# Products with M in one burst per group and layer, and another order of a network kernel's first microseconds

## The chip, the cores and the metric

The kernel runs on one core of a Trainium2 chip. The metric is device time in microseconds; lower is better. The kernel before was run four times: 3079.81, 3082.77, 3082.37 and 3082.63 us, median 3082.5 us.

## The reference

The input `x` holds 4 images of 32 by 32 positions and 16 channels, in float32. Four residual layers follow one another, each on a normalised copy of `x`:

```python
x = x + _L0_conv_ref(_gn(x), L0_conv_M, L0_conv_W, L0_conv_G)
x = x + _L1_conv_ref(_gn(x), L1_conv_M, L1_conv_W, L1_conv_G)
x = x + _L2_conv_ref(_gn(x), L2_conv_W0, L2_conv_b0, L2_conv_W1, L2_conv_b1, L2_conv_W2, L2_conv_b2)
x = x + _L3_conv_ref(_gn(x), L3_conv_M, L3_conv_Wp, L3_conv_G)
```

`_gn` normalises over the image and pairs of channels. Layers 0, 1 and 3 have the form

```python
first = jnp.einsum('ijyx,byxc->bijc', Msq, inputs)          # a 1024 x 1024 matrix
shifted = lax.conv_general_dilated(x_nchw, kern, STRIDES, PADDING)   # 1024*16 kernels of 3x3x16
diff = jax.nn.relu(inputs[:, None, None, :, :, :] - shifted)
second = L * jnp.einsum('ijyx,bijyxc->bijc', Wsq, diff)
return first - second
```

so that every output position has its own convolution of the whole image, whose result is weighed with a row of `W` and summed. Layer 2 is a pooling over intervals with two small dense steps; it matters here only as work beside the rest.

## The kernel before, in words

**Groups and phases.** The four images form two groups of two. The three big layers and two groups give six phases (L68), layer by layer, group 0 ahead of group 1. `conv_layer` (L431) works through one phase: 8 chunks of 128 output positions, 16 filters `f`, 2 images `b`, so 256 steps a phase and 1536 in all. A step is one PSUM tile `pc` of 128 by 1024: three slots of taps, each 64 rows deep in two halves that lie in different rows of the array (L457 to L467). Slots 0 and 1 multiply `raw` (the weights G as loaded, after a subtraction in place) with `im` (the shifted image, float32); slot 2 multiplies `W9` with `im9` (float32r). VectorE then clamps, weighs with the rows of W (tile `WT`) and sums, in one SCALAR_TENSOR_TENSOR `junk` (L471). There are three PSUM buffers for `pc`.

**Feeding.** A unit is 8 filters of a chunk (16 steps). `load_raw(u + 3)` is issued on SP's queue at step 2 of unit `u`, into four buffers; `prep(u + 1)` (L142) runs a tensor_tensor subtraction of `pick` on GpSimd (L150) and an ACT copy with a scale, `halve` (L123), and `prep_rest` adds VectorE's part, `halve_rest` (L126).

**Work beside the steps.** A generator `behind(phase)` (L487) holds the next phase's preparations; it is advanced by a count of steps that it yields itself. It holds the group norms, layer 2's `interval_layer` (L305: among others four transposes on VectorE L318, a scaled copy on ACT L322, a select on GpSimd L324), `before_conv` and `first_term` (L240), the products with M. The order of instructions on each engine is that of the recording; no scheduler rearranges them.

**The products with M.** `first_term` loads M of a layer in two halves of 2 MB (L247) into tile `MT`, which has one buffer. After a half is requested it waits 12 steps, then issues 32 products (4 tiles of 128 positions, 4 column strips of the array, each in two float32 passes; 16 program instructions), then requests the second half, waits 12 steps and issues the rest. Both halves add up in one PSUM bank `pf`. Two steps later VectorE transposes the bank and adds it to `X`. `first_term` is run six times.

**The first microseconds.** SP loads `XQ` (a copy of group 0 for the statistics), `im[0]` of image 0 in three transfers, one for each slot, the first `WT` chunk, the other six filters of the first `raw`, and image 1; ACT's queue loads the first two filters of `raw` (`F0 = 2`, L96). From `XQ` come the mean and the variance, each spread over the partitions by a product with `to_rows` (`first_stats`, L545, a multiply `by_batch` on VectorE and a product on TensorE). ACT takes the square root (L581), VectorE the reciprocal (L582), and then `normal` (L596: VectorE slots 0 and 1, ACT slot 2) and `sides` (L583: multiplications by 0 or 1 at the image's edges) make `im[0]`. The lines from L606 to L615 set the order. The first two filters are prepared by `prep(0, 0, F0, nc.vector)` (L579), ahead of the square root.

Of the kernel before, what the change touches and what calls it, by code (L numbers as in the profile page):

```python
# [8 lines left out]
F32 = mybir.dt.float32  # L9
# [5 lines left out]
P = 128  # L15
# [6 lines left out]
NT = NP // P  # L22
# [6 lines left out]
FU = 8  # L29
# [8 lines left out]
def net_kernel(ctx: ExitStack, tc: tile.TileContext, x, xq, xi, convs, iv_w, iv_b, out):  # L38
# [12 lines left out]
    nc = tc.nc  # L51
# [3 lines left out]
    wpool = ctx.enter_context(tc.tile_pool(name="wpool", bufs=2))  # L55
# [8 lines left out]
    def bank(name):  # L64
        return psum.tile([P, 512], F32, tag="one", bufs=2, name=name)
# [18 lines left out]
    def load_chunk(n):  # L84
        if n < n_chunks:
            t = n % NT
            chunks[n] = wpool.tile([P, NP], F32, tag="WT", name=f"WT_{n}")
            nc.sync.dma_start(chunks[n], convs[phases[n // NT][1]][1][t * P : (t + 1) * P, :])

    im = [const.tile([P, 3, GB, PITCH], F32, name=f"im{g}") for g in range(NG)]  # L90
# [2 lines left out]

    F0 = 2
    raws[0] = wpool.tile([P, 3, FU, P], F32, tag="raw", bufs=4, name="raw_0")
    nc.scalar.dma_start(raws[0][:, :, :F0], convs[0][2][0, 0][:, :, :F0])  # L96
    for slot in (0, 2, 1):
        nc.sync.dma_start(im[0][:, slot, 0], xi[0][:, slot])
    load_chunk(0)
    nc.sync.dma_start(raws[0][:, :, F0:], convs[0][2][0, 0][:, :, F0:])  # L100
    nc.sync.dma_start(im[0][:, :, 1], xi[1])
# [20 lines left out]
    def halve(dst, src, mask):  # L122
        nc.scalar.activation(dst, src, AF.Copy, scale=mask[:, 1:2])  # L123
# [15 lines left out]
        for y in (0, HP - 1):  # L139
            nc.gpsimd.dma_start(xs[g][:, y * HP : (y + 1) * HP], zero[:GC])  # L140

    def prep(u, at=0, to=FU, eng=nc.gpsimd):  # L142

        if u >= n_chunks * NU:
            return
        if at == 0:
            units[u] = (raws.pop(u), wpool.tile([P, FU, P], F32R, tag="W9", name=f"W9_{u}"))
        raw, W9 = units[u]
        f0 = u % NU * FU
        eng.tensor_tensor(  # L150
            raw[:, 1, at:to], raw[:, 1, at:to],
            pick[:, f0 + at : f0 + to].unsqueeze(2).to_broadcast([P, to - at, P]),
            ALU.subtract,
        )
        halve(W9[:, at:to], raw[:, 2, at:to], low_w)

    def prep_rest(u, at=0, to=FU):
        if u in units:
            raw, W9 = units[u]
            halve_rest(W9[:, at:to], raw[:, 2, at:to], low_w)  # L160
# [79 lines left out]
    def first_term(g, layer):  # L240


        xn = xns[g]
        ps = bank(f"pf_{g}{layer}")
        for half in range(2):
            mt = wpool.tile([P, NT // 2, 4, 256], F32, tag="MT", bufs=1, name=f"MT_{g}{layer}{half}")
            nc.sync.dma_start(mt, convs[layer][0][half])  # L247
            yield 12
            for k in range(NT // 2):
                pt = NT // 2 * half + k  # L250
                for j in range(4):
                    nc.tensor.matmul(  # L252
                        ps[32 * j : 32 * j + 32, :256], lhsT=xn[:, pt, :], rhs=mt[:, k, j, :],
                        start=pt == 0, stop=pt == NT - 1, tile_position=(0, 32 * j),
                    )
        yield 2
        ft = work.tile([P, NT * GC], F32, tag="fs", name=f"ft_{g}{layer}")
        nc.vector.transpose(ft, ps[:, : NT * GC])
        yield 1
        nc.vector.tensor_tensor(  # L260
            X[g], X[g], ft.rearrange("p (t m) -> p t m", t=NT), ALU.add
        )
        yield 1
# [167 lines left out]
    def conv_layer(phase, behind):  # L431
# [6 lines left out]
        for t in range(NT):  # L438
# [4 lines left out]
            for at, (f, b) in enumerate(steps):  # L443
# [3 lines left out]
                if at % (FU * GB) == (8 if u == 0 else 2):  # L447
                    prep(u + 1)
# [38 lines left out]
    def behind(phase):  # L487
        g, layer = phases[phase]
        if phase == 0:
            load_raw(1)  # L490
            load_raw(2)
            yield from rest_of_start()
            nc.scalar.dma_start(X[1], x[1])
            zeros(1)
            yield 1
            yield from constants()
        if phase + 1 < len(phases):
            g1, layer1 = phases[phase + 1]
            if layer1 == 2:
                yield from interval_layer(g1)  # L500
            yield from before_conv(g1, layer1)
            yield from first_term(g1, layer1)
        if phase == 0:
            yield from first_term(g, layer)
        if phase == len(phases) - 1:
            nc.sync.dma_start(out[1 - g], X[1 - g])
# [36 lines left out]
    s1 = const.tile([P, 1], F32, name="s1")  # L543

    def first_stats(src, name):  # L545

        ps = bank(f"ps_{name}")
        by_batch = work.tile([P, GB], F32, tag="by_batch", name=f"by_batch_{name}")
        nc.vector.tensor_scalar_mul(by_batch, own, src)
        nc.tensor.matmul(  # L550
            ps[:, :GB], lhsT=to_rows.rearrange("p k g s -> p (k g s)"), rhs=by_batch,
            start=True, stop=True,
        )
        return ps[:, :GB]

    nc.vector.tensor_reduce(s1, XQ, axis=AX.X, op=ALU.add)
    ps = bank("ps_own")
    nc.tensor.matmul(
        ps[:, :1], lhsT=to_own.rearrange("p q b c -> p (q b c)"), rhs=s1, start=True, stop=True
    )  # L560
    m = first_stats(s1, "m0")
    v = ident.rearrange("p (h q c) -> p q c h", h=2, q=4)
    nc.vector.tensor_reduce(pick, v[:, 0], axis=AX.X, op=ALU.add)
    low_w = rows_mask("low_w", ident.rearrange("p (h w k) -> p w h k", h=2, w=2)[:, 1:2])
# [9 lines left out]
    mean0 = const.tile([P, GB], F32, name="mean0")  # L574
    minus_mean0 = const.tile([P, GB], F32, name="minus_mean0")
    var = first_stats(s2, "v0")
    nc.vector.tensor_copy(mean0, m)
    nc.vector.tensor_scalar_mul(minus_mean0, m, -1.0)
    prep(0, 0, F0, nc.vector)  # L579
    rstd0 = const.tile([P, GB], F32, name="rstd0")  # L580
    nc.scalar.activation(rstd0, var, AF.Sqrt, bias=eps)  # L581
    nc.vector.reciprocal(rstd0, rstd0)  # L582
    def sides(eng, b, slot):  # L583

        v = im[0][:, slot, b].rearrange("p (y x) -> p y x", x=HP)
        if slot == 2:
            eng.memset(v[:, :, H - 1 : H], 0.0)
            eng.memset(v[64:, HI - 1, :H], 0.0)
        for side, at in (
            ("left", v[:, :, 0]), ("right", v[:, :, H - 1]),  # L590
            ("top", v[:, 0, :H]), ("bottom", v[:, HI - 1, :H]),
        ):
            if f"{side}{slot}" in keep:
                eng.tensor_scalar_mul(at, at, keep[f"{side}{slot}"])  # L594

    def normal(eng, b, slot):  # L596
        v = im[0][:, slot, b, :RUN]
        if eng is nc.scalar:
            eng.activation(v, v, AF.Identity, bias=minus_mean0[:, b : b + 1])
            eng.activation(v, v, AF.Copy, scale=rstd0[:, b : b + 1])  # L600
        else:
            eng.tensor_scalar(  # L602
                v, v, mean0[:, b : b + 1], rstd0[:, b : b + 1], op0=ALU.subtract, op1=ALU.mult
            )

    normal(nc.scalar, 0, 2)  # L606
    normal(nc.vector, 0, 0)
    sides(nc.vector, 0, 0)
    prep_rest(0, 0, F0)
    normal(nc.vector, 0, 1)  # L610
    sides(nc.vector, 0, 1)
    sides(nc.gpsimd, 0, 2)
    halve(im9[0][:, 0], im[0][:, 2, 0], low_x)
    halve_rest(im9[0][:, 0], im[0][:, 2, 0], low_x)
    prep(0, F0, FU)  # L615

    def rest_of_start():
# [92 lines left out]
```

## Time and profile before

| what | us |
|---|---|
| median of 4 runs | 3082.5 |
| profiled execution, its own time | 3079.81 |
| its span in the trace | 3078.1 |
| TensorE busy in the span | 3062.4 |
| VectorE busy | 2122.9 |
| GpSimd busy | 302.1 |
| ScalarE busy | 142.0 |

1.7 us of the profiled execution's time lie around the span. All four runs lie within 3.0 us, and the profiled one is the fastest of them. The page of the profile gives for each line its engine, its count, its busy time, the mean length of one and the idle time ahead of it with what ended it. The timeline gives a start, a length, an engine and a line for each instruction, in microseconds from the span's start. PEld is the weight load, which runs beside the products.

### The profile page before, as it was taken

What the parts mean: (1) busy time and instruction counts of PE and PEld (TensorE: products, weight loads), DVE (VectorE), ACT (ScalarE), POOL (GpSimd) and SP (SyncE); (2) the same over time, 40 slices, a digit from 0 to 9 for tenths busy, and PEclk for the clock granted to TensorE, in tenths of its full rate; (3) what the DMA queues carried; (4) which work ended last, traced back from release to release, by engine and by line L of the source; (5) the groups of instructions that cost most, each with busy time, mean ns of one, the idle gap of its engine ahead of it and who ended that gap; (6) DMA issues with size and microseconds to landing.
All of it is one profiled execution on the core that took longest, in us unless ns stands there. A gap on an engine that the chain in (4) does not pass through costs nothing.

```text
span 3078.1 us, 38112 instructions
## 1 busy us (share of the span) xinstructions
PE 3062.4 (99%) x15858; PEld 2071.1 (67%) x15858; DVE 2122.9 (69%) x3398; ACT 142.0 (5%) x145; POOL 302.1 (10%) x196
## 2 busy tenths in 40 slices
PE   8999999999999999999999999999999999999999
PEld 4555876758767766876775556685646578677776
DVE  6766666766666666666678776668877666666666
ACT  1000000000000000000000000000000000000000
POOL 3100000100000000000013310001330000000000
PEclk9999999999999999999999999999999999999999
DMA  3322112321111231111121113211113212121100
GB/s 144 126 103 77 67 48 76 99 95 49 52 72 48 71 125 71 53 55 62 48 76 48 69 59 116 76 48 61 57 48 126 76 48 71 48 76 49 69 28 2
DMA packets 36461, 215.20 MB, mean 70 GB/s; under 512 B 10432, under 2 KB 11456, under 8 KB 22592
## 3 DMA queue, kind: packets, MB, share of 16 engines
q1 hardware_dynamic: 29728, 207.65, 18.5%
q10 hardware_dynamic: 6432, 5.10, 0.7%
q8 instruction: 124, 2.03, 0.3%
q14 instruction: 49, 0.40, 0.0%
q0 software_dynamic: 128, 0.02, 0.0%
HBM read 211.77 MB, written 0.98 MB: 69 GB/s over the span
## 4 chain that ended last, share of the span: by engine, by line
PE 99%; DVE 0%; issue 0%; DMA 0%; ACT 0%; ACTq 0%
PE pc L461 98%; PE pf L252 1%; DVE junk L471 0%; DMA raw<-in_g 0%; PE ps_r L371 0%; PE ps_l L360 0%; DVE im L594 0%; PE ps_l L358 0%; DVE pp L318 0%; ACT L581 0%; ACT L123 0%; DVE im L602 0%; PE ps_y L422 0%; ACT W L123 0%; DVE W L126 0%
## 5 line engine op out<-in xcount | busy, mean ns | idle before, releaser
L461 PE MATMUL pc<-im,raw 64*128 64x512 f32 x12288 | 3001.5, 590 | 6.1 <-DVE im L594 4.3
L471 DVE SCALAR_TENSOR_TENSOR junk<-pc,WT 128x1024 f32<-128x1024 f32 x1536 | 1879.0, 1223 | 945.4 <-PE pc L461 939.9
L461 PEld LDWEIGHTS pc<-im,raw 64*128 64x128 f32 x12288 | 1712.5, 186 | 746.7 <-issue 425.8
L461 PE MATMUL pc<-im,W 64*128 64x512 f32 x3072 | 1709.5, 806 | 0.0
L461 PEld LDWEIGHTS pc<-im,W 64*128 64x128 f32 x3072 | 484.7, 186 | 227.6 <-issue 165.1
L150 POOL TENSOR_TENSOR raw<-raw,pick 128x1024 f32<-128x1024 f32 (+1 forms) x96 | 181.4, 1891 | 1918.4 <-DMA raw<-in_g 1790.0
L123 ACT ACTIVATE W<-raw,low_w 128x1024 fp32r<-128x1024 f32 (+1 forms) x97 | 110.6, 1140 | 2464.3 <-PE pc L461 2464.3
L126 DVE SCALAR_TENSOR_TENSOR W<-raw,low_w,W 128x1024 fp32r<-128x1024 f32 (+1 forms) x97 | 135.0, 1391 | 0.0
L471 DVE DVE_READ_ACCUMULATOR junk<-pc,WT 128x1 f32 x1536 | 126.7, 82 | 0.0
L391 POOL TENSOR_TENSOR dp_a<-ft_a,rt_r 128x1089 f32<-128x1089 f32 x16 | 39.0, 2446 | 75.5 <-DVE s_a L398 49.5
L391 POOL TENSOR_TENSOR dp_b<-ft_b,rt_r 128x1089 f32<-128x1089 f32 x16 | 37.1, 2324 | 94.6 <-ACT ft_b L384 47.7
L252 PE MATMUL pf<-MT,xn 128*32 128x256 f32 x384 | 23.2, 382 | 0.0
L182 POOL PARTITION_ALL_REDUCE sum_mc<-part_mc x6 | 2.7, 445 | 195.7 <-DVE part_mc L175 189.9
L398 DVE TENSOR_REDUCE s_b<-dp_b 128x33 f32<-128x1089 f32 x16 | 20.5, 1283 | 0.0
L398 DVE TENSOR_REDUCE s_a<-dp_a 128x33 f32<-128x1089 f32 x16 | 20.5, 1282 | 0.0
L252 PEld LDWEIGHTS pf<-MT,xn 128*32 128x32 f32 x384 | 11.3, 109 | 13.1 <-issue 6.9
L483 DVE TENSOR_TENSOR X<-X,acc 128x32 f32<-128x32 f32 x48 | 11.8, 247 | 1.5
L123 ACT ACTIVATE im<-im,low_x 128x1088 fp32r<-128x1088 f32 (+1 forms) x7 | 7.5, 1073 | 114.6 <-DMA im<-xs 110.3
L182 POOL PARTITION_ALL_REDUCE sum_mi<-part_mi x2 | 0.9, 445 | 116.6 <-DVE part_mi L175 116.6
L338 DVE TENSOR_TENSOR pp<-pp 64x1024 f32<-64x1024 f32 x10 | 12.1, 1212 | 0.0
L333 DVE TENSOR_TENSOR pp<-pp 64x1024 f32<-64x1024 f32 x10 | 12.1, 1211 | 0.0
L182 POOL PARTITION_ALL_REDUCE sum_vc<-part_vc x6 | 2.6, 441 | 88.4 <-DVE part_vc L175 82.4
(102 smaller groups left out, 141.4 us busy)
## 6 DMA issues: line engine op xcount, KB each, us to landing
raw<-in_g SPq DMA_DIRECT2D x95, 1536.0 KB, 6.6
WT<-in_w SPq DMA_DIRECT2D x48, 512.0 KB, 6.4
MT<-in_mt SPq DMA_DIRECT2D x12, 2048.0 KB, 7.8
im<-xs SPq DMA_DIRECT2D x60, 67.8 KB, 3.1
im<-xs ACTq DMA_DIRECT2D x60, 67.8 KB, 3.2
raw<-in_g SPq DMA_DIRECT2D x1, 1152.0 KB, 7.8
im<-in_xi SPq DMA_DIRECT2D x3, 272.0 KB, 4.5
im<-in_xi SPq DMA_DIRECT2D x1, 816.0 KB, 9.2
```

Of the source, the lines that this page charges most:

```text
L123: nc.scalar.activation(dst, src, AF.Copy, scale=mask[:, 1:2])
L126: nc.vector.scalar_tensor_tensor(dst, src, mask[:, 0:1], dst.bitcast(F32), op0=ALU.mult, op1=ALU.add)
L150: eng.tensor_tensor(raw[:, 1, at:to], raw[:, 1, at:to], pick[:, f0 + at : f0 + to].unsqueeze(2).to_broadcast([P, to - at, P]), ALU.subtract,)
L182: nc.gpsimd.partition_all_reduce(m, part, channels=P, reduce_op=bass_isa.ReduceOp.add)
L252: nc.tensor.matmul(ps[32 * j : 32 * j + 32, :256], lhsT=xn[:, pt, :], rhs=mt[:, k, j, :], start=pt == 0, stop=pt == NT - 1, tile_position= ...
L333: nc.vector.tensor_tensor(pp[k][:, :H, M:], a[:, :H, M:], a[:, s : H + s, M:], ALU.max)
L338: nc.vector.tensor_tensor(pp[k][:, :H, M:], a[:, :H, M:], a[:, :H, M - s : M - s + H], ALU.max)
L391: nc.gpsimd.tensor_tensor(t, ft[:, i, :].unsqueeze(1).to_broadcast([P, T1, T1]), rt, ALU.add,)
L398: nc.vector.tensor_reduce(s[:, i - 1, :], last, axis=AX.X, op=ALU.max)
L461: nc.tensor.matmul(ps[:, h, :], lhsT=w[:, f % FU, :], rhs=v[:, :, :H], start=slot == 0, stop=slot == 2,)
L471: nc.vector.scalar_tensor_tensor(junk, ps.rearrange("p h n -> p (h n)"), 0.0, chunks[n], op0=ALU.min, op1=ALU.mult, accum_out=acc[:, t, co ...
L483: nc.vector.tensor_tensor(X[g][:, t], X[g][:, t], acc[:, t], ALU.add)
```

## The change

Two things are changed.

`first_term` has one tile `MT` for the whole M of a layer, twice as large and still with one buffer. Both halves are requested one after the other, then 24 steps pass, then all 64 products are issued in one go. The count of steps up to the end of `first_term` (28) is the same.

The first microseconds are ordered differently. Image 0 comes in one transfer of 816 KB instead of three of 272 KB. The variance's product stands ahead of the mean's; the mean's `by_batch` multiply moves behind the variance's. The subtraction for the first two filters goes from VectorE to GpSimd, and `prep(0, 0, F0)` with its ACT copy stands behind the square root and not ahead of it. VectorE does slot 0 and slot 1 with their sides first and `prep_rest(0, 0, F0)` after them.

```diff
+    nc.sync.dma_start(im[0][:, :, 0], xi[0])
     nc.scalar.dma_start(raws[0][:, :, :F0], convs[0][2][0, 0][:, :, :F0])
-    for slot in (0, 2, 1):
-        nc.sync.dma_start(im[0][:, slot, 0], xi[0][:, slot])
...
-        eng.tensor_tensor(
+        nc.gpsimd.tensor_tensor(
...
+        mt = wpool.tile([P, NT, 4, 256], F32, tag="MT", bufs=1, name=f"MT_{g}{layer}")
+        for half in range(2):
+            nc.sync.dma_start(mt[:, NT // 2 * half : NT // 2 * (half + 1)], convs[layer][0][half])
+        yield 24
         ps = bank(f"pf_{g}{layer}")
-        for half in range(2):
-            mt = wpool.tile([P, NT // 2, 4, 256], F32, tag="MT", bufs=1, name=f"MT_{g}{layer}{half}")
-            nc.sync.dma_start(mt, convs[layer][0][half])
-            yield 12
-            for k in range(NT // 2):
-                pt = NT // 2 * half + k
-                for j in range(4):
-                    nc.tensor.matmul(
-                        ps[32 * j : 32 * j + 32, :256], lhsT=xn[:, pt, :], rhs=mt[:, k, j, :],
-                        start=pt == 0, stop=pt == NT - 1, tile_position=(0, 32 * j),
-                    )
+        for pt in range(NT):
+            for j in range(4):
+                nc.tensor.matmul(
+                    ps[32 * j : 32 * j + 32, :256], lhsT=xn[:, pt, :], rhs=mt[:, pt, j, :],
+                    start=pt == 0, stop=pt == NT - 1, tile_position=(0, 32 * j),
+                )
...
-    m = first_stats(s1, "m0")
...
     var = first_stats(s2, "v0")
+    m = first_stats(s1, "m0")
     nc.vector.tensor_copy(mean0, m)
     nc.vector.tensor_scalar_mul(minus_mean0, m, -1.0)
-    prep(0, 0, F0, nc.vector)
...
+    prep(0, 0, F0)
     normal(nc.scalar, 0, 2)
-    normal(nc.vector, 0, 0)
-    sides(nc.vector, 0, 0)
+    for slot in range(2):
+        normal(nc.vector, 0, slot)
+        sides(nc.vector, 0, slot)
+    sides(nc.gpsimd, 0, 2)
     prep_rest(0, 0, F0)
-    normal(nc.vector, 0, 1)
-    sides(nc.vector, 0, 1)
-    sides(nc.gpsimd, 0, 2)
```

More of the change, by code (lines that the diff above doesn't have):

```diff
@@ L140, in zeros, with prep @@
             nc.gpsimd.dma_start(xs[g][:, y * HP : (y + 1) * HP], zero[:GC])
-    def prep(u, at=0, to=FU, eng=nc.gpsimd):
+    def prep(u, at=0, to=FU):
         if u >= n_chunks * NU:
```

## The prediction

> **What bounds the kernel now.** I read the page first, then the chain of work that ended last, then timelines of three places: the start, a burst of M products, and the one place where TensorE waited after the start.
>
> ```profile
> span 3078.1 us, 38112 instructions
> PE 3062.4 (99%) x15858; PEld 2071.1 (67%) x15858; DVE 2122.9 (69%) x3398; ACT 142.0 (5%) x145; POOL 302.1 (10%) x196
> ...
> PE 99%; DVE 0%; issue 0%; DMA 0%; ACT 0%; ACTq 0%
> ```
>
> TensorE is the bound all along: 99% of the chain is its own. Only two things move the time: what TensorE does per step or burst, and the 15.7 us (3078.1 - 3062.4) in which it does nothing. Of those, some 12.5 lie ahead of 13.18 us; 1.8 lie at 2106 us; the rest is VectorE's last step.
>
> The start, from the timeline (start, length, engine, line):
>
> ```profile
> 5.60 1.28 ACT L123 ACT_TABLE_LOAD   x1 [5.60 <-DMA raw<-in_g]
> ...
> 6.20 0.59 PE L550 MATMUL ps_v<-by_batch_v,to_rows 128*128 128x2 f32 x2 [1.23 <-DVE by_batch_v L549]
> ...
> 6.90 0.51 ACT L123 ACTIVATE W<-raw,low_w 128x256 fp32r<-128x256 f32 x1
> ...
> 7.42 1.28 ACT L581 ACT_TABLE_LOAD   x1
> ...
> 8.72 0.26 ACT L581 ACTIVATE rstd<-ps_v,eps 128x2 f32<-128x2 f32 x1
> ...
> 10.53 2.08 PE L461 MATMUL pc<-im,raw 64*128 64x512 f32 x4 [3.74 <-DVE im L594]
> ...
> 11.17 1.50 POOL L150 TENSOR_TENSOR raw<-raw,pick 128x768 f32<-128x768 f32 x1 [0.41 <-DMA raw<-in_g]
> ...
> 11.37 1.75 DVE L594 TENSOR_SCALAR im<-im,kept 128x16 f32<-128x16 f32 x3
> ...
> 13.18 2.08 PE L461 MATMUL pc<-im,raw 64*128 64x512 f32 x4 [0.57 <-DVE im L594]
> ```
>
> The variance is ready at 6.79 (6.20 + 0.59), but ACT takes its root at 8.72: ahead of it in ACT's order stand the copy for the first two filters and a second table load, because that copy comes first and loads another table. The first three sides of slot 1 take 1.75 us, those of slot 0 took 0.66: the first of the three (1.33 us by its line's longest) ends when GpSimd's subtraction ends. So slot 0's products start at 10.53 and slot 1's, from which on TensorE runs without a break, at 13.18.
>
> A burst of M (VectorE's steps around it; the same distances stand at the other eleven, within 0.4 us where VectorE had extra work):
>
> ```profile
> 168.46 1.22 DVE L471 SCALAR_TENSOR_TENSOR junk<-pc,WT 128x1024 f32<-128x1024 f32 x1 [0.72 <-PE pc L461]
> ...
> 170.30 1.45 PEld L252 LDWEIGHTS pf<-MT,xn 128*32 128x32 f32 x32 [0.57 <-issue]
> ...
> 170.42 1.22 DVE L471 SCALAR_TENSOR_TENSOR junk<-pc,WT 128x1024 f32<-128x1024 f32 x1 [0.73 <-PE pc L461]
> ...
> 172.17 0.30 PEld L461 LDWEIGHTS pc<-im,raw 64*128 64x128 f32 x4 [0.41 <-issue]
> ...
> 174.44 1.22 DVE L471 SCALAR_TENSOR_TENSOR junk<-pc,WT 128x1024 f32<-128x1024 f32 x1 [2.79 <-PE pc L461]
> ```
>
> A step without a burst is 1.96 us (168.46 to 170.42), one with it 4.02 (170.42 to 174.44): a burst costs 2.06.
>
> **Part 1, M in one burst.** Nothing is taken out of the sum of products: 384 stay 384. The chain of waits gives 1.86 us for each 32, so 2.06 - 1.86 = 0.20 us is what going in and out of a burst costs. In the order of the built program the 64 products of a group and layer stand in a row, so six of twelve such changes go: 6 x 0.20 = **1.2 us less**. Ends: 0, and from the weight loads' idle time around a burst (0.57 + 0.41, less twice the 0.24 that a step has anyway, 0.5) 6 x 0.5 = 3.0. I take 0.2, for it is measured on the path.
>
> The loads: 2 MB land 7.8 us (median) after issue, at worst 11.2, both halves so in about 16 to 22 us, and the burst is 24 x 1.96 = 47 us behind. The halves stand on SP's queue ahead of a WT or a raw load, which they delay by as much; a raw load is issued at step 2 of unit u and used at step 2 of u + 2, 63 us later. If this cover were gone, TensorE would wait for the landing itself, up to 11 us a group; the margin is 25 us. On the other hand SP no longer stands waiting for the first 32 products (58.8 us in three waits up to 300 us now); behind it stood raw loads with the same 63 us of room, so this is worth nothing. VectorE is empty handed for 3.7 us in a row and not twice 1.9; it waits 0.73 a step anyway. PSUM: the bank is taken later and given back at the same step.
>
> **Part 2, the first microseconds.** With the root first, ACT has one table load, which waits for nothing in the new order and lies at about 1.5 to 2.8 us. VectorE's `by_batch` for the mean (0.23 long, 0.20 on its neighbours) moves behind the variance: by_batch of the variance is due at 5.72 instead of 5.92. But GpSimd now does the subtraction of the first two filters when they land, at 5.60; by its row for 768 columns (1.50) that is 0.50, and a small VectorE multiply may stand until it ends, as the sides at 11.37 did: I take 6.1. Then, with the rows' lengths and 0.05 between engines: 0.23 + 0.05 + 0.59 to the variance, root at 7.0 to 7.3; beside it the mean's multiply 0.23, its product 0.59, the copies 0.2 to 8.15; the reciprocal 0.17 to 8.3. VectorE's order makes the mean the later of the two now. From the start of `normal` to the first product it was 1.32 (9.21 to 10.53), so slot 0's products start at 9.6. Image 0's transfer is needed at 8.2; its three parts landed within 4.6 us of issues up to 2.2, one transfer of the same bytes ahead of the same others in the same queue should be there by 7.
>
> Slot 1 is then `normal` 0.56 and sides 0.66 behind slot 0's, at 10.8, ahead of the landing of raw's rest at about 11.1, which starts GpSimd's long subtraction: the 1.33 us hold is gone. TensorE needs slot 1 after two pairs at the slow clock, 2 x 0.855 (the distance of weight loads up to 18.89), at 11.3. Slot 2 needs ACT's two passes from 8.2 (1.52 long), GpSimd's clearing 0.35, ACT's copy 0.75 and VectorE's 0.48 + 0.78: about 12.0; it is due at 13.0. Now slot 0 is done in 1.71 and TensorE goes on without a break from 9.6.
>
> The clock: weight loads come every 0.855 us up to 18.89 and every 0.43 after about 19.2, 6.0 after the unbroken start at 13.18. At 19.2 before has done 1.71 + 5.9 = 7.6 us of work at the slow clock. With 6.0 again, after is at full clock at 15.6, with 6.0 done; the other 1.6 takes 0.8: level at 16.4, so **2.8 us less**. Ends: if the clock counts from the first product (10.53 to 19.2 is 8.7), 1.4 less; if it takes only the 3.65 us of the restart shown below, 4.0 less; if GpSimd holds VectorE by as much as in that place (3.0 us more than usual) when the variance is due, slot 1 comes at 13.9 and 0.7 us is lost. I take 2.8, as the nearest row is the same start.
>
> A rule beside a row: here the load at 7.42 takes 1.28, and the root follows at 8.72. The Trainium skill, "ScalarE: Activation LUTs", "What ACT_TABLE_LOAD costs", has 1283 ns for the load and some 1380 more for a drain at each switch of sets. By that page the switch that goes would be worth 1.4 more, and the whole some 5.4 instead of 4.0; the row shows no such drain, and I go by the row.
>
> **Sum.** 1.2 + 2.8 = 4.0 less: 3079.81 becomes 3075.8 for an execution like the profiled one. That one is 2.7 below the median; I take the 4.0 off the median: **3078.5 us**. That is no more than 0.13%; 0.2%, or 6.2 us, is about what a measurement of this kernel can tell from no change.
>
> **What may lie over it.** One place explains why runs differ by 2.7:
>
> ```profile
> 1588.88 1.28 DVE L126 SCALAR_TENSOR_TENSOR W<-raw,low_w,W 128x1024 fp32r<-128x1024 f32 x1
> 1588.93 2.37 POOL L324 TENSOR_SCALAR_AFFINE_SELECT pp<-pp 64x1024 f32<-64x1024 f32 x1 [15.15 <-ACT pp L322]
> ...
> 2102.40 4.27 DVE L126 SCALAR_TENSOR_TENSOR W<-raw,low_w,W 128x1024 fp32r<-128x1024 f32 x1
> 2102.45 1.27 POOL L324 TENSOR_SCALAR_AFFINE_SELECT pp<-pp 64x1024 f32<-64x1024 f32 x1 [15.10 <-ACT pp L322]
> ...
> 2107.87 3.65 PE L461 MATMUL pc<-im,raw 64*128 64x512 f32 x8 [1.76 <-DVE junk L471]
> ```
>
> In group 1's interval layer VectorE and GpSimd start within 0.05 us of one another and VectorE loses: 4.27 instead of 1.28. TensorE stands still 1.76 us and comes back at half clock (0.50 to 0.53 of it up to 2111.5). In group 0 the same pair went the other way and cost nothing. From 2098.30 to 2153.00 there are 26 steps, 54.70 - 26 x 1.962 = 3.7 us lost. The change doesn't touch this place, but each execution may lose here none, once or twice.
>
> **The rivals.**
> *One loss fewer:* if the runs of the changed kernel lose 3.7 us once where the median of before lost it twice, 3078.5 - 3.7 = 3074.8, faster. For it: 0.05 us decides, and the four runs differ by about such a step. Against: the order at this place is the same, so the same odds.
> *The start brings nothing:* the mean's later product and GpSimd's hold eat what the table load gives. Only M's 1.2 is left: 3081.3. For it: the 4.27 row; against: 1.93 us between variance and root are gone at once.
> *M brings nothing,* as the array's change of shape is hidden or is paid by the product: 3079.7. That the burst isn't one is excluded by the built order.
> *Slower:* a burst of 3.7 us lowers TensorE's clock. The products with M use 32 columns and rows of 256 elements and may count as little activity; a burst of 1.9 is maybe too short for it. Price: after the stall the clock was at half for 3.65 us, 1.8 us lost; six times, 11.0: 3078.5 + 11.0 = 3089.5. It turns the sign from 0.7 us a burst, and 0.2% from 1.7. Against: the granted clock is 1.00 in every window around the bursts, and the step after a burst is as short as others (174.44 to 176.41). The trace has no burst of 3.7.
> The row says that a stand of 1.76 us was enough. The Trainium skill, "TensorE: Matmul & The Clock Gate", "What's actually happening", wants about 3.4 us of an idle window for a drop and as much of a busy one for the way back; a burst of 3.7 would be longer than its window and two of 1.9 are not, so if that page's monitor saw the bursts as idle, it would speak against this change with about that price.
>
> **How the numbers follow.** Forecast 3078.5: 0.50. One loss fewer, 3074.8: 0.20. Start without gain, 3081.3: 0.17. M without gain, 3079.7: 0.07. Slower, 3089.5: 0.06. Faster by over 0.2% (below 3076.3) is the second alone: 0.20; slower by over 0.2% (above 3088.7) the last: 0.06; within it the rest: 0.74. The range takes in all but the last: from 3074.8 less 0.8 for the start's better end, 3074.0, to the start's worse end (0.7 lost, 1.2 won, 3082.0) and some of the runs' own spread, 3083.0.
>
> **What would show it.** One table load ahead of 5 us; the root by 7.3; slot 0's products by 9.6 and no wait of TensorE up to the second step; full clock by about 15.6 (3.4 us earlier). Bursts of 64, 3.72 long, with one gap; a step with a burst 5.9 us instead of 4.0 twice, and clock 1.00 after it. L126 at the two interval layers: 1.28 or 4.27 tells how many losses the execution had. I am wrong if TensorE waits at a burst, if the clock drops after one, or if slot 0's products come later than 10.5.

## The result, and the profile after

The changed kernel takes **3077.0 us** (median of 34 runs, 3072.2 to 3078.28) against 3082.2 us (54 runs, 3076.8 to 3083.5) of the kernel before: ratio 0.9983, 95% interval 0.9978 to 0.9988, so 5.2 us or 0.17% less. Forecast were 3078.5 us and 4.0 us less.

The profiled execution of the changed kernel took 3076.75 us. The page's head:

```profile
span 3075.0 us, 38107 instructions
...
PE 3059.2 (99%) x15858; PEld 2005.2 (65%) x15858; DVE 2126.4 (69%) x3397; ACT 141.1 (5%) x144; POOL 301.4 (10%) x197
```

TensorE is the bound as before. The start, in the timeline of the changed kernel (start, length, engine, line):

```profile
1.47 1.28 ACT L578 ACT_TABLE_LOAD   x1 [1.47 <-PEq L695]
...
5.14 0.61 POOL L149 TENSOR_TENSOR raw<-raw,pick 128x256 f32<-128x256 f32 x1 [3.56 <-DVE XQ L565]
5.16 0.87 DVE L568 SCALAR_TENSOR_TENSOR squares<-XQ 128x256 f32<-128x256 f32 x1
...
6.99 0.26 ACT L578 ACTIVATE rstd<-ps_v,eps 128x2 f32<-128x2 f32 x1 [4.23 <-PE ps_v L548]
...
7.90 0.16 DVE L575 COPY mean<-ps_m 128x2 f32<-128x2 f32 x1 [0.68 <-PE ps_m L548]
...
8.23 0.56 DVE L599 TENSOR_SCALAR im<-im,mean,rstd 128x542 f32<-128x542 f32 x1
...
9.55 3.78 PE L459 MATMUL pc<-im,raw 64*128 64x512 f32 x8 [1.69 <-DVE im L591]
...
13.41 1.88 PE L459 MATMUL pc<-im,raw 64*128 64x512 f32 x8
```

One table load is left, off the path; the root comes 1.7 us earlier (8.72 before); slots 0 and 1 are one group of eight products, without the break before 13.18. What takes the root's place as the last to come is the mean (7.90). Beside GpSimd's subtraction VectorE's `squares` is 0.87 long (0.42 before, where GpSimd has no work there). The weight loads reach their short distance, the sign of the full clock, at 13.4. The fourth step's first weight load is at 17.09, before at 20.95: 3.86 us.

The first burst of M in the same trace, with VectorE's steps around it:

```profile
188.08 1.23 DVE L469 SCALAR_TENSOR_TENSOR junk<-pc,WT 128x1024 f32<-128x1024 f32 x1 [0.35 <-PE pc L459]
...
189.93 3.18 PEld L250 LDWEIGHTS pf<-MT,xn 128*32 128x32 f32 x64 [0.57 <-issue]
...
190.04 1.22 DVE L469 SCALAR_TENSOR_TENSOR junk<-pc,WT 128x1024 f32<-128x1024 f32 x1 [0.73 <-PE pc L459]
...
195.79 1.22 DVE L469 SCALAR_TENSOR_TENSOR junk<-pc,WT 128x1024 f32<-128x1024 f32 x1 [4.52 <-PE pc L459]
```

From 190.04 to 195.79 it is 5.75, less a step of 1.96: a burst of 64 costs 3.79, two of 32 cost 4.12. That is 0.33 a group and layer, 2.0 for six. The table by stretches has the burst in its second row and the steps after it in its third (length, busy time of the engines, granted clock, DMA share, GB/s):

```profile
186.00:189.90 3.90, 3.90 (x22) 1.62 (x18) 2.97 (x5) 0.00 (x0) 0.00 (x0) 1.00 0.00 0
189.90:193.50 3.60, 3.60 (x66) 1.98 (x64) 1.23 (x2) 0.00 (x0) 0.00 (x0) 1.00 0.02 5
193.50:197.40 3.90, 3.90 (x24) 1.97 (x22) 1.23 (x2) 0.00 (x0) 0.00 (x0) 1.00 0.71 227
```

TensorE is busy throughout, its clock stays at 1.00, and the next step takes the usual 1.96 (195.79 to 197.75). The moments at which the granted clock changes, which the trace keeps, lie at none of the six bursts: the rival of a clock that falls after a long burst is gone.

The table of waits of the changed kernel (us in all, times, longest) and the timeline show that this execution lost at both interval layers, the profiled one of before only at the second:

```profile
PE pc L459 <- DVE junk L469: 3.5, 2, 1.8
```

```profile
1583.60 4.27 DVE L125 SCALAR_TENSOR_TENSOR W<-raw,low_w,W 128x1024 fp32r<-128x1024 f32 x1
1583.64 1.27 POOL L322 TENSOR_SCALAR_AFFINE_SELECT pp<-pp 64x1024 f32<-64x1024 f32 x1 [15.35 <-ACT pp L320]
1584.90 1.89 POOL L149 TENSOR_TENSOR raw<-raw,pick 128x1024 f32<-128x1024 f32 x1
...
1589.07 2.76 PE L459 MATMUL pc<-im,raw 64*128 64x512 f32 x8 [1.77 <-DVE junk L469]
```

VectorE's instruction is recorded 0.04 us ahead of GpSimd's, and ends only after two of GpSimd's. Counting 26 steps on from 1579.49 (to 1634.25) gives 54.76 - 26 x 1.962 = 3.75 us lost; from 2097.19 (to 2150.26) 2.06. The two differ by the clock, here after the first and after the second stand (what decides is in the last section):

```profile
1591.00:1592.00 1.00, 1.00 (x4) 0.45 (x4) 0.69 (x2) 0.00 (x0) 0.00 (x0) 0.50 0.00 0
...
2108.00:2109.00 1.00, 1.00 (x8) 0.55 (x6) 0.90 (x3) 0.00 (x0) 0.00 (x0) 1.00 0.00 0
```

So the spans add up roughly: -3.86 (start) - 2.0 (bursts) + 3.75 + 2.06 - 3.7 (two losses instead of one) = -3.75; measured -3.1 (3078.1 to 3075.0). By the first interval layer the two traces agree with it to 0.1 us (VectorE's transposes start at 1580.64 instead of 1585.93, 5.29 less). The other 0.7 us lie right behind it, at the interval layer's products `ps_r`: the 15 steps of VectorE around them take 31.62 us before (1633.86 to 1665.48) and 32.43 after (1632.28 to 1664.71). What makes them dearer the traces don't show.

### The profile page after: what moved, and what is told of

Same layout as the page of the kernel before. It is cut to its first block, busy times and chain, and to the rows that moved or that the text cites. A ratio compares the mean times of both kernels' runs of the same rounds, so it can differ in the third digit from the quotient of the medians.

```text
span 3075.0 us, 38107 instructions
## 1 busy us (share of the span) xinstructions
PE 3059.2 (99%) x15858; PEld 2005.2 (65%) x15858; DVE 2126.4 (69%) x3397; ACT 141.1 (5%) x144; POOL 301.4 (10%) x197
## 4 chain that ended last, share of the span: by engine, by line
PE 99%; DVE 1%; issue 0%; POOL 0%; POOLq 0%
PE pc L459 98%; PE pf L250 1%; DVE junk L469 0%; PE ps_r L369 0%; PE ps_l L358 0%; DVE pp L316 0%; PE ps_l L356 0%; DVE squares L568 0%; PE ps_y L420 0%; DVE im L591 0%; PE ps_m L548 0%; PE ps_v L548 0%; DVE im L599 0%; DVE kept L539 0%; DVE to_own L523 0%
## 5 line engine op out<-in xcount | busy, mean ns | idle before, releaser
L459 PEld LDWEIGHTS pc<-im,raw 64*128 64x128 f32 x12288 | 1681.5, 186 | 705.8 <-issue 424.4
L459 PE MATMUL pc<-im,W 64*128 64x512 f32 x3072 | 1659.0, 806 | 0.0
## 6 DMA issues: line engine op xcount, KB each, us to landing
MT<-in_mt SPq DMA_DIRECT2D x12, 2048.0 KB, 11.6
```

Source lines behind the costliest of these rows:

```text
L459: nc.tensor.matmul(ps[:, h, :], lhsT=w[:, f % FU, :], rhs=v[:, :, :H], start=slot == 0, stop=slot == 2,)
```

## The experiments

My theory: both parts gain, M by fewer changes of burst and the start by the root; over them lies the meeting of VectorE and GpSimd in the interval layers, which costs an execution 0, 2.1 or 3.7 us at each of two places. Rivals: all of it is the start; all of it is fewer losses; the long burst costs clock. Twelve kernels ran, in three sets of four, each set on one chip (another one each time) with the kernel before beside it, which had medians of 3079.89, 3082.44 and 3082.18 us. To take the meeting away, "shifted" kernels move the interval layer's transposes, copy and select two steps later and keep all that follows in place:

```diff
             nc.gpsimd.memset(t, -BIG)
-        yield 3
+        yield 5
...
-        yield 4
+        yield 2
         k = 0
```

| kernel | median us (range, runs) | ratio to before, 95% interval |
|---|---|---|
| e1 M alone | 3076.37 (3073.17 to 3079.8, 11) | 0.9987, 0.9979 to 0.9996 |
| e2 start alone | 3077.32 (3073.72 to 3081.5, 11) | 0.9989, 0.9980 to 0.9997 |
| e3 before, shifted | 3075.85 (3075.21 to 3076.3, 11) | 0.9984, 0.9975 to 0.9993 |
| e4 changed, shifted | 3071.18 (3070.38 to 3072.42, 6) | 0.9970, 0.9958 to 0.9981 |
| e5 M alone, shifted | 3073.89 (3072.89 to 3074.66, 8) | 0.9973, 0.9963 to 0.9983 |
| e6 start alone, shifted | 3073.29 (3072.32 to 3074.67, 7) | 0.9974, 0.9963 to 0.9984 |
| e7 = e4, M in quarters | 3076.37 (3075.51 to 3077.74, 11) | 0.9982, 0.9973 to 0.9991 |
| e8 = e4, mean first | 3071.02 (3069.93 to 3071.69, 5) | 0.9964, 0.9952 to 0.9977 |
| e9 = e4, three transfers | 3070.33 (3069.53 to 3071.36, 5) | 0.9964, 0.9952 to 0.9977 |
| e10 = e8, three transfers | 3069.59 (3069.3 to 3070.9, 5) | 0.9963, 0.9950 to 0.9975 |
| e11 = e3, root first | 3072.17 (3071.42 to 3072.85, 6) | 0.9969, 0.9958 to 0.9981 |
| e12 = e3, slots first | 3074.65 (3073.35 to 3075.73, 11) | 0.9978, 0.9969 to 0.9987 |

**e1, M alone.** The diff of `first_term` without the rest.

> Only the products with M are changed: one tile for the whole matrix, one burst of 64 per group and layer; the first microseconds are as before. My theory (a change of burst costs TensorE a fixed time, and both parts add up): a step with a burst is 5.75 us in the trace, as in the changed kernel, and twice 4.02 in the kernel before, so 0.33 x 6 = 2.0 us less than before: 3080.2 median; clock 1.00 after each burst. Rival A (the gain is all in the start): within 0.5 us of before. Rival B (the long burst lowers the clock): longer by 1.8 us a burst, 11 us.

3.5 us less, with an interval of 1.2 to 6.5: the part gains by itself, rivals A and B fall. For its size the interval is too wide.

**e2, start alone.** The rest of the diff, `first_term` as before.

> Only the first microseconds are changed; M is multiplied in two bursts as before. My theory: slot 0's products start at 9.5 to 9.6 us and TensorE goes on without a break; 1.4 to 4.0 us less than before, by the moment at which the clock rises; median 3079.3, that is 2.9 less. Rival A: all of the changed kernel's 5.2 us. Rival C (the difference is one of collisions in the interval layers alone): within 0.5 us of before once the two places are counted out.

2.6 us less, interval 0.9 to 6.2. This too gains by itself; that it isn't all of the 5.2 the interval doesn't show (e5 and e6 do). Its runs lie 7.8 us apart, and its profiled execution lost once (1.8 us of waiting), that of e1 twice (3.5).

**e3 and e4, the shift.** The diff above, on the kernel before and on the changed one.

> The kernel before, with the interval layer's transposes, scaled copy and select two steps later (yield 3 becomes 5, and the yield after the select 4 becomes 2, so that all that follows stands where it stood). My theory: VectorE's L126 and GpSimd's select no longer meet, L126 is 1.28 us in both places, TensorE doesn't wait after the start; one or two losses of 2.1 to 3.75 us go, so 3 to 6 us less than before, median 3077.5, and the runs lie closer together. Rival (the 4.27 us come from another cause than the meeting, or move to the next place): the time stays within 1 us of before.

> The changed kernel with the same two steps' shift. My theory: what the shift gives adds to what the change gives, so as much under the changed kernel as the shifted kernel before is under the kernel before, 3 to 6 us: median 3072.5; and it stands under the shifted kernel before by 2.0 (bursts) + 1.4 to 4.0 (start) = 3.4 to 6.0. Rival C (the change gives its time only by fewer collisions): within 1 us of the shifted kernel before.

The theory holds. In e3's timelines of VectorE and of GpSimd the two are 5 us apart and the first is 1.28 again (in the second interval layer, at 2101.54, too):

```profile
1588.03 1.28 DVE L126 SCALAR_TENSOR_TENSOR W<-raw,low_w,W 128x1024 fp32r<-128x1024 f32 x1
...
1590.37 1.77 DVE L318 STREAM_TRANSPOSE pp<-xi 32x256 f32<-32x256 f32 x4
```

```profile
1593.36 1.28 POOL L324 TENSOR_SCALAR_AFFINE_SELECT pp<-pp 64x1024 f32<-64x1024 f32 x1 [19.64 <-ACT pp L322]
```

TensorE waits for nothing after the start in e4, and the runs of e3 lie within 1.1 us where those of before beside it spread over 5.3. Between e3 and e4, on the same chip, it is 3075.85 - 3071.18 = 4.7 us, which is what the change is worth where the meeting is out of play. Rival C (only fewer losses) falls.

**e5 and e6, the parts on the shifted kernel.**

> The shifted kernel before (3075.85 in the last comparison, its runs within 1.1 us) with the long burst alone. My theory: 6 x 0.33 = 2.0 us less, 3073.8. Rival A (the gain is all in the start): 3075.8. Forecast's own price, 0.2 a burst: 3074.6.

> The shifted kernel before with the new first microseconds alone. My theory: what is left of the 4.7 us between the two shifted kernels, 2.7 less: 3073.2; and the two parts together make up the 4.7. Rival (they are not independent): the two parts' sum is off by over 1 us.

Against e3: 2.0 for M and 2.6 for the start, together 4.5 of the 4.7, so the parts are independent to within the 1 us that the rival names. e3 ran in the set before, on another chip.

The traces allow a sharper comparison, without the start and without the meeting: from VectorE's `junk` of the fifth step to that of the last. It is 3045.07 us in e6 and 3045.10 in e11 (below), both with two bursts, and 3043.05 to 3043.08 in e4, e5, e8, e9 and e10, with one. So M's gain is 2.0 us, the 0.33 for each of six that the trace shows, not my 0.20.

But e3 takes 3044.32, 0.75 less than e6 with the same products. The difference lies at `ps_r` again: the 15 steps there take 31.62 us in e3, as in before, and 32.42 in e4, e5 and e6. If other executions do as the profiled ones, each of these three pays some 0.75 us there; then the start alone is worth about 3.3 and not 2.6, and that the medians of e3 and e5 lie 2.0 apart, M's full gain, is chance. One trace for each kernel doesn't decide that.

**e7, M in quarters.**

```diff
-        yield 24
+        yield 21
...
         for pt in range(NT):
+            if pt in (2, 4, 6):
+                yield 1
```

> The shifted changed kernel with each burst of M cut in four, with a step between each two (21 steps of waiting, then three more, in place of 24). My theory (each way into and out of a burst costs TensorE 0.33): 6 x 3 x 0.33 = 5.9 us more than the shifted changed kernel, 3077.1. Rival (the long burst gains by its loads, both halves requested together): no change, 3071.2.

5.2 us more than e4 (on another chip) and not 5.9. By the traces each of the six places costs 0.99 more, 5.9 in all, and `ps_r` gives 0.8 back (31.60 for its 15 steps, as in before). A burst of 16 products in e7's timeline, by VectorE's steps:

```profile
188.02 1.22 DVE L471 SCALAR_TENSOR_TENSOR junk<-pc,WT 128x1024 f32<-128x1024 f32 x1 [0.73 <-PE pc L461]
...
191.18 1.23 DVE L471 SCALAR_TENSOR_TENSOR junk<-pc,WT 128x1024 f32<-128x1024 f32 x1 [1.93 <-PE pc L461]
```

3.16 - 1.96 = 1.20 us. With 2.06 for 32 and 3.79 for 64 this is a line: 0.054 us a product and 0.34 for each burst. The rival of the loads falls: e7 requests both halves together too.

**e8, mean first.** On e4: the mean's product ahead of the variance's, the subtraction for the first two filters on VectorE ahead of its wait for the root.

```diff
+    m = first_stats(s1, "m0")
     v = ident.rearrange("p (h q c) -> p q c h", h=2, q=4)
...
     var = first_stats(s2, "v0")
-    m = first_stats(s1, "m0")
...
+    prep(0, 0, F0, nc.vector, copy=False)
     rstd0 = const.tile([P, GB], F32, name="rstd0")
...
-    prep(0, 0, F0)
+    halve(units[0][1][:, :F0], units[0][0][:, 2, :F0], low_w)
     normal(nc.scalar, 0, 2)
```

> The shifted changed kernel with the mean's product ahead of the variance's again, and the subtraction for the first two filters on VectorE, ahead of its wait for the root; the root stays ahead of ACT's copy. My theory (root first is what the start gains by; the mean's place and GpSimd's hold cost): root at 6.8 to 7.1, slot 0's products at 8.7 and not 9.55 to 10.1; 0.9 to 1.4 us less than the shifted changed kernel, 3070.0. Rival (the mean's later product is what gains): 1 to 2 us more, 3072.5.

A miss: 0.2 less (e4 on another chip), by the median. The root came at 6.83 as expected, but the next to be late was image 0:

```profile
7.12 0.17 DVE L581 RECIPROCAL rstd<-rstd 128x2 f32<-128x2 f32 x1 [0.52 <-ACT rstd L580]
...
8.03 0.56 DVE L601 TENSOR_SCALAR im<-im,mean,rstd 128x542 f32<-128x542 f32 x1 [0.74 <-DMA im<-in_xi]
```

The single transfer had taken 6.7 us from its issue. It holds the changed start in some executions too; in e4's profiled one the same line was

```profile
8.80 0.56 DVE L599 TENSOR_SCALAR im<-im,mean,rstd 128x542 f32<-128x542 f32 x1 [0.70 <-DMA im<-in_xi]
```

**e9 and e10, three transfers,** on e4 and on e8:

```diff
-    nc.sync.dma_start(im[0][:, :, 0], xi[0])
...
+    for slot in (0, 2, 1):
+        nc.sync.dma_start(im[0][:, slot, 0], xi[0][:, slot])
```

> The shifted changed kernel (3071.2) with image 0 in three transfers again, slots 0, 2, 1, as before. In the traces the single transfer lands 6.1 to 7.5 us after its issue, at 7.3 to 8.7, and VectorE's first normalisation stands ready at 8.1 to 8.2; the three parts of before landed 4.1 to 4.6 us after issue. My theory (the single transfer is at times the last to come): slot 0's products at 9.5 in each execution and not up to 10.1; 0 to 0.7 us less, 3070.8. Rival (the single transfer helps by its shorter issue): 0.5 us more.

> Mean's product first, VectorE subtracts for the first two filters, root first on ACT (with one transfer 3071.0, its first normalisation held by the image to 8.03), now with image 0 in three transfers. My theory (the transfer hid what the mean's place gives): normalisation at 7.3, slot 0's products at 8.7; 0.5 to 1.0 us less than with one transfer, 3070.3; it would be the fastest of all. Rival (slot 1 or the other six filters' weights come too late to use it): 3071.0.

e9 is 0.85 under e4 (another chip), e10 0.74 under e9 (same chip) and has the lowest median of all, 3069.59 us, some 12.6 under before in its set. Both steps are of the size of the runs' own spread: the ranges of e4 and e9, and of e9 and e10, overlap. What the traces show is the order of the start. In e10 the normalisation follows the reciprocal at once:

```profile
7.12 0.17 DVE L582 RECIPROCAL rstd<-rstd 128x2 f32<-128x2 f32 x1 [0.52 <-ACT rstd L581]
7.32 0.56 DVE L602 TENSOR_SCALAR im<-im,mean,rstd 128x542 f32<-128x542 f32 x1
...
8.64 3.78 PE L461 MATMUL pc<-im,raw 64*128 64x512 f32 x8 [1.85 <-DVE im L594]
```

**e11, root first,** on e3; nothing else of the new start:

```diff
-    prep(0, 0, F0, nc.vector)
+    prep(0, 0, F0, nc.vector, copy=False)
...
+    halve(units[0][1][:, :F0], units[0][0][:, 2, :F0], low_w)
     normal(nc.scalar, 0, 2)
```

> The shifted kernel before (3075.85) with one thing alone from the new start: ACT's copy for the first two filters stands behind the root. Mean first, three transfers, VectorE's subtraction and its order as before. My theory (the root behind the copy and its second table load is what held the start): one table load ahead of 5 us, root at 6.84, slot 0's products at 8.7 instead of 10.5, slot 1 without GpSimd's hold at 10.4; 2.7 to 4 us less: 3072.5, as good as the whole new start (3073.3) or better. Rival (VectorE's order, slots ahead of W, is what gains): at most 1 us less, 3075.

3.7 us less than e3, where the whole new start gives 2.6 (e3, e6 and e11 ran on three chips). So the root's place is what gains, and the rest of the new start together gives about 1 us back. Root and first products in e11's trace (weight loads for the second line):

```profile
6.83 0.26 ACT L582 ACTIVATE rstd<-ps_v,eps 128x2 f32<-128x2 f32 x1 [4.07 <-PE ps_v L551]
...
8.64 0.50 PEld L462 LDWEIGHTS pc<-im,raw 64*128 64x128 f32 x4 [1.93 <-DVE im L595]
```

**e12, slots first,** on e3:

```diff
-    prep_rest(0, 0, F0)
     normal(nc.vector, 0, 1)
     sides(nc.vector, 0, 1)
     sides(nc.gpsimd, 0, 2)
+    prep_rest(0, 0, F0)
```

> The shifted kernel before (3075.85) with VectorE's order alone from the new start: slots 0 and 1 with their sides ahead of the first two filters' W. My theory: the root still comes at 8.7 and slot 0's products at 10.5; slot 1 comes up to 0.5 us earlier, or not at all where GpSimd's subtraction holds its sides: 0 to 0.9 less, 3075.4. Rival (this order is what gains): 2.6 less, 3073.3.

1.2 less, a little over what I expected. In its trace the sides are held by GpSimd as before and slot 1 comes no earlier:

```profile
11.46 1.93 DVE L594 TENSOR_SCALAR im<-im,kept 128x16 f32<-128x16 f32 x3
...
13.44 2.08 PE L461 MATMUL pc<-im,raw 64*128 64x512 f32 x4 [0.35 <-DVE im L594]
```

TensorE's break is shorter (0.35, in e3 0.57). The rest of the 1.2 is the clock: full clock comes at 16.67, 3.2 us after 13.44, and in e3 at 19.19, 5.8 us after 13.36. From the fifth step to the last both take 3044.32. The last section shows that this time differs from execution to execution, so it is no gain of the order by itself. Why e12's median has it too, over 11 runs on another chip, stays open.

## Why the prediction was right, point by point

- **What bounds it.** Right: no wait of TensorE's came or went but at the start and in the interval layers. The split of the 15.7 us was misread: 9.5 of them lie ahead of 13.18, not 12.5, for TensorE was busy for 3.7 there; 1.8 lie at 2106, and 4.4 behind TensorE's last product (3073.67). The sum doesn't use it.
- **M in one burst, 1.2 us.** The mechanism was right, the size was off: 2.0 (six times 0.33, in the traces). The step that failed is "2.06 - 1.86 = 0.20". I took the chain's 1.86 for 32 products as their bare cost; it holds part of the way in and out. The bare cost is 0.054 x 32 = 1.72, and a burst's own cost 0.34, as e7's third size shows. The other end that I gave, 0.5, was the idle time of the weight loads, and too much.
- **Loads and queues, nothing.** Right in its outcome: the clock was 1.00 and TensorE was busy around the bursts. Both halves requested together land after 11.6 us (median) and 17.0 at most, instead of 7.8 and 11.2; the 47 us cover it.
- **The start, 2.8 us.** Measured 2.6 (e3 to e6). Its steps: root 7.0 to 7.3 (6.99 to 7.25), reciprocal's end 8.3 (8.19), slot 0 at 9.6 (9.55), no break (none). GpSimd's hold cost what I had put down, here on `squares`; in e2, e4, e6, e7 and e9 `squares` is 0.43 and the multiply after it 0.45 to 0.66 instead of 0.23, as forecast. Full clock by 15.6: by the weight loads it was 13.4 in this execution, 3.9 us after the first product, and between 3.2 (e8) and some 6.2 us (e2, e4) in the others with an unbroken start, so 6.0 was near the late end of what happens. That 2.8 and 2.6 lie so close is in part luck: mostly by the clock, single pairs of traces have the fifth step 0.6 (e5 to e4) to 4.4 us (e3 to e6) earlier, and of what e6 won some 0.75 was lost at `ps_r`, which I had not foreseen.
- **"should be there by 7"** of image 0's transfer was wrong: in the runs with one transfer it landed 6.1 to 7.5 us after its issue at 1.24, so at 7.3 to 8.7, and held the changed start by 0.6 us in two of the traces (e2, e4). I had taken the landing of one third for that of the whole.
- **The mean as the later of the two** was right. With the subtraction's place it costs slot 0's products 0.89 us (9.53 in e9, 8.64 in e10); the 0.74 us between the medians of five runs each is no more than an indication.
- **The rival "one loss fewer"** named the right thing: these losses are most of the spread (3072.2 to 3078.28 among the changed kernel's runs). The median moved without it: the change itself is 4.7, and the other 0.5 of the 5.2 is within the interval of the comparison (3.7 to 6.8).
- **The row against the page** on the table load: the trace has no gap for a drain, for the load starts at 7.42 where the copy ends (6.90 + 0.51), and the root at 8.72 where the load ends (7.42 + 1.28). e11's 3.7 us come with the root 1.9 us earlier, slot 1's hold gone and TensorE without its break, so its time alone can't exclude one.

## What to carry to other kernels

Where one engine is busy 99% of the time, look for what it pays per change and not per product: here a product costs 0.054 us whatever the burst's size, and each way into and out of one 0.34 us. In a start-up chain, look at what stands ahead of the longest dependent chain on its engine: here a copy and the table load that it drew in held the root by 1.9 us. When one link is shortened, name the next that comes last (mean, then image, then products) and see whether it can be shortened too. When runs of one kernel lie some microseconds apart, find the place in the trace where two engines meet within 0.05 us; moving one of them by two steps was worth nearly as much as the whole change (4.0 against 4.7).

## What the runs showed of the hardware that I had not expected

- A VectorE multiply-add with two SBUF inputs that is recorded 0.04 to 0.05 us ahead of a GpSimd select may lose to it, and to the GpSimd instruction queued right behind: 4.27 us for 1.28, six of eight times in the traces of before, the changed kernel, e1 and e2. Twice it won, and the select took 2.37 us instead of 1.27. The order of the recorded starts doesn't tell which of them goes first.
- The clock changes on a grid of 3.41 us. In the trace of before it rises at 19.10, falls at 2108.05 and rises at 2111.47; in that of the changed kernel it does so at 13.19, 1590.15 and 1593.56. The distances are 612, 1, 462 and 1 times 3.4133 us, and the weight loads bear the first rises out to within 0.4 us. Where the grid lies against the kernel's start differs from execution to execution. The column of the granted clock reads 1.00 ahead of the first change, where the weight loads are 0.855 apart and not 0.43; after a stand in mid-run it shows the half clock (0.50).
- In all 14 traces the clock rises at the end of the first stretch of this grid in which TensorE worked for 2.87 us (e8) or more; 2.84 (before and e3) were not enough. So the time from the start of unbroken products to full clock was anything from 2.9 us (e8) to 6.0 us (e4).
- The clock fell at the end of a stretch in which TensorE stood for 1.50 us (e6, at the end of its run) or more, and not after 1.44 (e4, likewise). A stand of 1.76 us at an interval layer lay in one stretch three times (before, the first of the changed kernel, e2), and cost 3.7 us. Three times an edge of the grid cut it (into 0.55 and 1.20 us in the second of the changed kernel; both of e1), the clock stayed, and it cost 2.1.
- The Trainium skill, "TensorE: Matmul & The Clock Gate", "What's actually happening", has a window of 3.4 us that runs free of the kernel; the grid agrees. An estimate from that page, with one whole window of work needed, would be a rise 3.4 to 6.8 us after a start; the traces have 2.9 to 6.0. For a fall the same page has an idle window of about 3.4 us; here 1.76 us of standing in one were enough.
- One transfer of 816 KB landed at 7.3 to 8.7 us. As three of 272 KB in the same queue the same bytes landed 4.1 to 5.4 us after their issues at 1.2 to 2.2, the last of them by 6.8 (e9) to 7.6 (e1).
